# An attention block with modulation and experts: the loads and the first norms of its start in another order

## The chip, the cores and the metric

The kernel runs on one core of one Trainium2 chip. A core has TensorE (PE in the profile; its weight loads are the row PEld), VectorE (DVE), ScalarE (ACT), GpSimd (POOL) and SyncE (SP). Each works through its own instructions in order and waits on semaphores for the others. Transfers are issued by SP, ScalarE or GpSimd and run on 16 shared DMA engines. The metric is the device time of one execution in microseconds; lower is better.

## What is computed

The input x has 8 batches of 1024 tokens with 256 features. A small vector c per batch is turned into six rows of modulation (shift, scale and gate for each of two halves), which frame an attention with 16 heads of 64 and a layer of eight experts:

```python
mod = (_silu(c) @ wmod).reshape(8, 6, 1, -1)
sa, ca, ga, sb, cb, gb = (mod[:, i] for i in range(6))
ga = (2 * (ga >= 0) - 1) * jnp.maximum(jnp.abs(ga), 0.25)      # gb likewise
h = _layernorm(x) * (1 + ca) + sa
x = x + ga * attention(h, w_qkv, w_o)                          # softmax over 1024 keys, 16 heads
h = _layernorm(x) * (1 + cb) + sb
x = x + gb * experts(h, router_w, router_b, w1, b1, w2, b2)    # each expert takes its 512 best tokens
```

For the start of the kernel it matters who needs what. The first product (the values of the first heads of batch 0) needs the normalized x of batch 0, the shift and scale columns sa and ca, and the weights of a few heads. The gates and the second half's shift and scale are needed only when a whole batch has been through attention, and the router's weights and the experts' biases later still.

## The kernel before, in words

All arithmetic is in float32 apart from small helpers. Attention runs over units: a unit is one batch, one pair of heads and 512 of its 1024 queries (`unit`, L303). Per unit, eight chunks of 128 keys are multiplied to scores (`scores_mm`, L306), copied out by ScalarE (L322) while VectorE keeps the running maximum (L327), the maximum is turned and subtracted (L334 to L372), ScalarE takes the exponential (L375), TensorE multiplies with the values (L384), and GpSimd adds up the denominators (L403). Each batch also needs its x normalized and turned (`ln_task`: load L225, statistics L231, norm L234, transposes and modulation L243), and query, key and value products (`qk_task` L270, `v_task` L287).

The order of all this is written out by hand. `at(g, where, f)` puts a function into a table at step g, and the loop under `tc.manual_schedule()` (L647) runs through the steps, four to a unit; step 0 issues the first scores. Steps below 0 are the run-up: the loop starts at g = -28; batch 0's four pairs of token tiles are put at steps -23, -20, -17 and -14 (L604), each with its load four steps, its statistics two steps and its norm one step earlier; products of the first heads start at step -9 (L609 to L613).

Ahead of the loop stands a setup. SP issues rw, rb, b1 (L85, L87, L96) and then the whole of wmod (`wm`, L119). c becomes SiLU(c) in `silu`, is turned to `sT`, and is multiplied with wm in two forms: as columns, which give shift and scale of attention for each batch (`modT`, L134 to L141), and as rows, which give the two gates and the second shift and scale (`mrow`, L143 to L160), stored to DRAM as `mod_d` and `gb_d`. The setup has pools of its own, whose memory is given back before attention's pools are opened; so the query, key and value weights (`wq`, six transfers, L204) and `wo` (L208) are issued by ScalarE only after the setup's last use. They take the setup's place in memory.

A tile of a pool with a tag and `bufs` takes one of as many rotating buffers, and a new tile waits until the last use of the buffer that it takes is over. In PSUM, `ps_m` has a single buffer (tag "mm"), through which pass the transposes of the norm, the query, key and value products, the denominators and the output products. DMA completions are counted on eight semaphores in turn, so a transfer can also wait for the one eight places ahead of it.

The norm of one pair of tiles (`ln_norm`) takes rstd from two small GpSimd instructions (`rstd_of`, L166 and L168) and two GpSimd instructions for the norm itself (L238). `ln_out` makes 16 transposes on TensorE (L252) and two VectorE instructions that apply shift and scale (L257).

Of the kernel before, what the change touches and what calls it, by code (L numbers as in the profile page):

```python
# [28 lines left out]
F32 = mybir.dt.float32  # L29
BF16 = mybir.dt.bfloat16  # L30
I32 = mybir.dt.int32
AF = mybir.ActivationFunctionType
ALU = mybir.AluOpType
AX = mybir.AxisListType
PSUM = bass.MemoryType.PSUM
DRAM = bass.MemoryType.DRAM

P = 128
# [4 lines left out]
def adaln_block(  # L43
# [15 lines left out]
    nc = tc.nc  # L59
    B, S, D = x.shape  # L60
    H, _, _, N = w_qkv.shape
    E, _, F = w1.shape
    K = 512
    KC = D // P
    NT = S // P
# [7 lines left out]
    scale = 1.0 / N**0.5  # L73
# [4 lines left out]
    ident = const.tile([P, P], F32, name="ident")  # L78
# [3 lines left out]
    mhalf = const.tile([P, 1], F32, name="mhalf")  # L82
    nc.gpsimd.memset(mhalf, -0.5)
    rw = const.tile([P, KC, E], F32, name="rw")
    nc.sync.dma_start(rw, router_w.rearrange("(k p) e -> p k e", p=P))  # L85
    rb = const.tile([P, E], F32, name="rb")
    nc.sync.dma_start(rb, router_b.rearrange("(o e) -> o e", o=1).to_broadcast([P, E]))  # L87
    ident_b = const.tile([P, P], BF16, name="ident_b")
    nc.vector.tensor_copy(ident_b, ident)

# [2 lines left out]
    for j in range(2):  # L93
        nc.vector.memset(three[j * N : j * N + 3, :], 1.0)
    b1_sb = const.tile([P, E, FC], F32, name="b1_sb")
    nc.sync.dma_start(b1_sb, b1.rearrange("e (f p) -> p e f", p=P))  # L96

    scores = const.tile([P, KT, E, NTT // KT], F32, name="scores")
    modT = const.tile([P, 2 * KC, B], F32, name="modT")
# [10 lines left out]
    mod_d = dram.tile([B, 3 * D], F32, name="mod_d")  # L110
    gb_d = dram.tile([B, D], F32, name="gb_d")
    rows_d = dram.tile([B * S, WIDE], F32, name="rows_d")


    with tc.tile_pool(name="setup", bufs=1) as sp, tc.tile_pool(
        name="setup_ps", bufs=2, space=PSUM
    ) as spp:
        wm = sp.tile([P, KC, 6 * D], F32, name="wm")
        nc.sync.dma_start(wm, wmod.rearrange("(k p) m -> p k m", p=P))  # L119
        c_sb = sp.tile([B, D], F32, name="c_sb")  # L120
        nc.scalar.dma_start(c_sb, c)
        sig = sp.tile([B, D], F32, name="sig")
        nc.scalar.activation(sig, c_sb, AF.Exp, scale=-1.0)
        nc.vector.tensor_scalar_add(sig, sig, 1.0)
        nc.vector.reciprocal(sig, sig)
        silu = sp.tile([B, D], F32, name="silu")
        nc.vector.tensor_mul(silu, c_sb, sig)
        sT = sp.tile([P, KC, B], F32, name="sT")
        for k in range(KC):
            pt = spp.tile([P, B], F32, tag="small", name=f"pt{k}")  # L130
            nc.tensor.transpose(pt, silu[:, k * P : (k + 1) * P], ident[:B, :B])
            nc.vector.tensor_copy(sT[:, k, :], pt)

        for m in range(2 * KC):  # L134
            pm = spp.tile([P, B], F32, tag="small", name=f"pm{m}")
            for k in range(KC):
                nc.tensor.matmul(
                    pm, wm[:, k, m * P : (m + 1) * P], sT[:, k, :],
                    start=(k == 0), stop=(k == KC - 1),
                )  # L140
            nc.vector.tensor_scalar_add(modT[:, m, :], pm, 1.0 if m >= KC else 0.0)  # L141

        mrow = sp.tile([B, 4 * D], F32, name="mrow")  # L143
        for h in range(2):
            pr = spp.tile([B, 2 * D], F32, tag="row", name=f"pr{h}")
            for k in range(KC):
                nc.tensor.matmul(
                    pr, sT[:, k, :], wm[:, k, (2 + 2 * h) * D : (4 + 2 * h) * D],
                    start=(k == 0), stop=(k == KC - 1),
                )  # L150
            nc.vector.tensor_copy(mrow[:, 2 * h * D : (2 * h + 2) * D], pr)
        nc.vector.tensor_scalar_add(mrow[:, 2 * D : 3 * D], mrow[:, 2 * D : 3 * D], 1.0)
        for i in (0, 3):
            g = mrow[:, i * D : (i + 1) * D]
            sign = sp.tile([B, D], F32, name=f"sign{i}")
            nc.vector.tensor_scalar(sign, g, 0.0, 2.0, op0=ALU.is_ge, op1=ALU.mult)
            size = sp.tile([B, D], F32, name=f"size{i}")
            nc.vector.scalar_tensor_tensor(size, g, -1.0, g, op0=ALU.mult, op1=ALU.max)
            nc.vector.tensor_scalar_max(size, size, 0.25)
            nc.vector.scalar_tensor_tensor(g, sign, -1.0, size, op0=ALU.add, op1=ALU.mult)  # L160
        nc.sync.dma_start(mod_d, mrow[:, : 3 * D])
        nc.sync.dma_start(gb_d, mrow[:, 3 * D :])

    def rstd_of(pool, mv, n, name):
        ve = pool.tile([P, n], F32, tag="ve", name=f"ve_{name}")
# [16 lines left out]
    PB = 16  # L182
# [4 lines left out]
    wp = attn.enter_context(tc.tile_pool(name="wts", bufs=1))  # L187
    work = attn.enter_context(tc.tile_pool(name="work", bufs=2))
    small = attn.enter_context(tc.tile_pool(name="small", bufs=4))
# [2 lines left out]
    ps_av = attn.enter_context(tc.tile_pool(name="ps_av", bufs=1, space=PSUM))  # L192
    ps_m = attn.enter_context(tc.tile_pool(name="ps_m", bufs=1, space=PSUM))

    wq = wp.tile([P, KC, 3, H, N], F32, name="wq")
    wo = wp.tile([P, NP, D], F32, name="wo")

    parts_of = [wp.tile([P, 4, 2, N], BF16, name=f"parts{i}") for i in range(2)]
    for t in parts_of:
        nc.vector.memset(t, 0.0)  # L200

    for a in (2, 1, 0):
        for k in range(KC):
            nc.scalar.dma_start(  # L204
                wq[:, k, a],
                w_qkv[:, a, k * P : (k + 1) * P, :].rearrange("h p n -> p h n"),
            )
    nc.scalar.dma_start(wo, w_o.rearrange("(i p) d -> p i d", p=P))  # L208

    hTs, mods, qks, vs, oTs = {}, {}, {}, {}, {}  # L210
    tops, turned, rows_of, less, probs, sums, avs = {}, {}, {}, {}, {}, {}, {}
# [3 lines left out]
    def at(g, where, f, *args):  # L215
        steps.setdefault((g, where), []).append((f, args))
# [6 lines left out]
    ln_x = {}  # L223
# [7 lines left out]
    def ln_stats(b, t):  # L231
        ln_x[b, t] = ln_x[b, t], stats_of(small, ln_x[b, t], 2, f"a{b}_{t}")

    def ln_norm(b, t):  # L234
        xt, mv = ln_x[b, t]
        rs = rstd_of(small, mv, 2, f"a{b}_{t}")
        for i in range(2):
            nc.gpsimd.tensor_scalar(  # L238
                xt[:, i, :], xt[:, i, :], mv[:, i, 0:1], rs[:, i : i + 1],
                op0=ALU.subtract, op1=ALU.mult,  # L240
            )
# [21 lines left out]
    def ln_task(b, t, g):  # L263
        at(g - 4, "load", ln_load, b, t)
        at(g - 2, "post", ln_stats, b, t)
        at(g - 1, "pool", ln_norm, b, t)
        at(g, "m2", ln_out, b, t)


    def qk_task(b, p, i):  # L270
        a, half = (1, i) if i < 2 else (0, i - 2)
        if half == 0:
            qks[b, p, a] = work.tile([P, S], F32, tag="qk"[a], name=f"qk{a}_{b}_{p}")
        pq = ps_m.tile([P, 512], F32, tag="mm", name=f"pq{b}_{p}_{i}")
        sl = slice(half * 512, half * 512 + 512)
        for k in range(KC):
            for m in range(2):
                nc.tensor.matmul(  # L278
                    pq[m * N : (m + 1) * N, :], wq[:, k, a, 2 * p + m, :], hTs[b][:, k, sl],
                    start=(k == 0), stop=(k == KC - 1),  # L280
                )
        if a == 0:
            nc.scalar.mul(qks[b, p, a][:, sl], pq, scale)  # L283
        else:
            nc.scalar.copy(qks[b, p, a][:, sl], pq)  # L285

    def v_task(b, g, t):  # L287
        if t == 0:
            vs[b, g] = work.tile([P, NT, 4 * N], F32, tag="v", name=f"v{b}_{g}")
        pv = ps_m.tile([P, 2, 4 * N], F32, tag="mm", name=f"pv{b}_{g}_{t}")  # L290
        for i in range(2):
            for k in range(KC):
                for m in range(2):
                    t0 = (2 * t + i) * P + m * N
                    nc.tensor.matmul(  # L295
                        pv[m * N : (m + 1) * N, i, :], hTs[b][:, k, t0 : t0 + N],
                        wq[:, k, 2, 4 * g : 4 * g + 4, :],
                        start=(k == 0), stop=(k == KC - 1),
                    )
        nc.scalar.copy(vs[b, g][:, 2 * t : 2 * t + 2, :], pv)  # L300
# [300 lines left out]
        return g  # L601

    for t in range(NT // 2):
        ln_task(0, t, -23 + 3 * t)  # L604
        ln_task(1, t, free_slot(39 + 4 * t, True))
    for b in range(B):
        for p in range(NP):
# [13 lines left out]
        if b + 1 < B:  # L621
# [3 lines left out]
            for t in range(NT):  # L625
                g = free_slot(64 * (b + 1) + 19 + 4 * t, True)
# [3 lines left out]
                if t % 2:  # L630
                    g = free_slot(g + 2, True)
                    at(g, "m2", out_turn, ps_m, b, t - 1)
                    g = free_slot(g + 1)
# [7 lines left out]
            at(4 * u + 12, "m2", den_out, u)  # L641
    for b in range(B):
        at(64 * b + 30, "load", gates, b)
    for t in range(NT):
        at(4 * NSU + (3 if t < NT // 2 else 4), "load", last_load, t)

    with tc.manual_schedule():  # L647
        g = -28
        while g < 4 * NSU + LAG or steps:
            u, gm = divmod(g, 4)  # L650
            run(g, "load")
# [36 lines left out]
        b = B - 1  # L688
# [83 lines left out]
    with tc.tile_pool(name="search", bufs=2) as se, tc.tile_pool(  # L772
        name="pos", bufs=1
    ) as po_, tc.tile_pool(name="se_ps", bufs=2, space=PSUM) as sps, tc.tile_pool(
        name="pos_ps", bufs=1, space=PSUM
    ) as pps:
        for dst, pattern, mult in (
# [3 lines left out]
            i = po_.tile(list(dst.shape), I32, name=f"i_{dst.name}")  # L781
# [246 lines left out]
```

## Time and profile before

| | us |
| --- | --- |
| median of 3 runs | 3648.16 |
| lowest and highest | 3646.65 and 3648.54 |
| the profiled execution | 3645.84 |
| its span | 3644.1 |

| line | what | instructions | mean ns of one |
| --- | --- | --- | --- |
| L403 | POOL adds up denominators | 762 | 2371 |
| L372 | VectorE subtracts the maximum | 1024 | 1209 |
| L375 | ScalarE exponential | 1024 | 1057 |
| L322 | ScalarE copies scores | 1024 | 1018 |
| L313 | TensorE scores | 4096 | 613 |
| L384 | TensorE values | 4096 | 593 |
| L278 | TensorE queries and keys | 2048 | 605 |

The profile's page gives the busy time of each engine, then the span in 40 slices of equal length with the busy share of each engine in tenths, the clock that TensorE was granted, and the traffic. Busy matmul time is pipelined time: a full row says that TensorE always has something in progress. The timeline lists instructions in order of time; behind each stands, in brackets, how long its engine had been idle and what ended that. The mean granted clock of the execution was 0.979 of full speed.

### The profile page before, as it was taken

How to read it: one execution, taken by the hardware profiler on the slowest of the kernel's cores; microseconds unless marked ns; L12 is line 12 of the kernel's file. 1: busy time of each engine (PE TensorE's matmuls, PEld its weight loads, DVE VectorE, ACT ScalarE, POOL GpSimd, SP SyncE). 2: the span in 40 equal slices, each digit the busy share in tenths (PEclk: the TensorE clock that was granted, in tenths of full speed). 3: DMA queues.
4: the chain of work that ended last, by engine and by line, in shares of the span. 5: the costliest groups of instructions: out<-in, count | busy, mean ns of one | idle time of the engine just before them, and what ended most of it. 6: DMA issues, size and time to landing. Idle time of an engine off the chain costs nothing. (4 is left out here: it accounts for less than half of the span.)

```text
span 3644.1 us, 54310 instructions
## 1 busy us (share of the span) xinstructions
PE 3467.5 (95%) x20670; PEld 1461.3 (40%) x20670; DVE 2902.9 (80%) x3647; ACT 2431.7 (67%) x2978; POOL 2668.6 (73%) x1545
## 2 busy tenths in 40 slices
PE   5999999999999999999999999999999999982898
PEld 2333334334343444344343343344434334442565
DVE  3888888888888888888888888888888888857442
ACT  1777777777777777777777777777777777740111
POOL 1678777887788778888788888887888787851232
PEclk8999999999999999999999999999999999995999
DMA  3010002111120112011210113111211112133332
GB/s 76 7 39 27 24 31 58 49 38 45 45 62 30 52 48 66 29 45 45 62 52 29 51 50 62 30 50 46 62 38 43 46 48 59 51 85 122 93 99 41
DMA packets 189045, 185.40 MB, mean 51 GB/s; under 512 B 48856, under 2 KB 167144, under 8 KB 188656
## 3 DMA queue, kind: packets, MB, share of 16 engines
q1 hardware_dynamic: 159856, 156.62, 15.1%
q0 software_dynamic: 7168, 12.72, 1.7%
q10 hardware_dynamic: 21760, 12.59, 1.3%
q8 instruction: 163, 2.67, 0.3%
q14 instruction: 98, 0.80, 0.1%
HBM read 127.06 MB, written 63.21 MB: 52 GB/s over the span
## 5 line engine op out<-in xcount | busy, mean ns | idle before, releaser
L403 POOL TENSOR_TENSOR acc<-acc,p 128x1024 f32<-128x1024 f32 x762 | 1806.5, 2371 | 360.0 <-ACT p L375 327.0
L322 ACT COPY p<-s 128x1024 f32<-128x1024 f32 x1024 | 996.4, 1018 | 421.7 <-PE s L313 415.0
L372 DVE TENSOR_TENSOR p<-p,less 128x1024 f32<-128x1024 f32 x1024 | 1206.5, 1209 | 32.6 <-PE less L369 30.0
L327 DVE TENSOR_TENSOR top<-top,s 128x1024 f32<-128x1024 f32 x768 | 936.6, 1220 | 260.3 <-ACT p L322 219.3
L375 ACT ACTIVATE p<-p 128x1024 f32<-128x1024 f32 x1024 | 1041.8, 1057 | 74.7 <-DVE p L372 74.4
L313 PE MATMUL s<-qk,qk 64*128 64x512 f32 x4096 | 1025.8, 613 | 35.2 <-DVE parts L350 32.1
L384 PE MATMUL av<-p,v 128*64 128x512 f32 x4096 | 967.1, 593 | 1.8 <-ACT oT L393 1.8
L313 PEld LDWEIGHTS s<-qk,qk 64*128 64x128 f32 x4096 | 358.9, 187 | 527.4 <-issue 237.8
L278 PE MATMUL pq<-hT,wq 128*64 128x512 f32 x2048 | 495.9, 605 | 2.7 <-ACT qk L285 1.4
L384 PEld LDWEIGHTS av<-p,v 128*64 128x64 f32 x4096 | 280.6, 137 | 461.4 <-issue 366.9
L400 POOL TENSOR_TENSOR acc<-p,p 128x1024 f32<-128x1024 f32 x127 | 301.6, 2375 | 176.2 <-ACT p L375 176.2
L278 PEld LDWEIGHTS pq<-hT,wq 128*64 128x64 f32 x2048 | 124.2, 136 | 342.7 <-issue 211.4
L295 PE MATMUL pv<-wq,hT 128*64 128x256 f32 x2048 | 250.7, 387 | 2.6 <-ACT qk L283 1.4
L953 ACT ACTIVATE h<-ph,b_sb 128x512 f32<-128x512 f32 x64 | 44.0, 687 | 276.1 <-PE ph L949 276.1
L342 DVE TENSOR_REDUCE tt<-tt 128x8 f32<-128x1024 f32 x128 | 157.4, 1229 | 67.6 <-PE tt L334 67.5
L494 PE MATMUL po<-wo,ot 128*64 128x256 f32 x1792 | 205.7, 382 | 0.0
L295 PEld LDWEIGHTS pv<-wq,hT 128*64 128x64 f32 x2048 | 136.5, 137 | 155.7 <-issue 66.5
L327 DVE TENSOR_TENSOR top<-p,s 128x1024 f32<-128x1024 f32 x128 | 155.7, 1217 | 32.3 <-ACT p L322 32.3
L300 ACT COPY v<-pv 128x512 f32<-128x512 f32 x128 | 75.0, 586 | 148.4 <-PE pv L295 148.4
L334 PEld LDWEIGHTS tt<-ident,top 128*128 128x128 f32 x1024 | 109.6, 140 | 107.2 <-DVE top L327 107.2
L465 POOL TENSOR_TENSOR oT<-oT,rb 128x1024 f32<-128x1024 f32 x63 | 150.0, 2381 | 3.0 <-issue 3.0
L494 PEld LDWEIGHTS po<-wo,ot 128*64 128x64 f32 x1792 | 123.5, 137 | 66.2 <-issue 9.4
(161 smaller groups left out, 2442.8 us busy)
## 6 DMA issues: line engine op xcount, KB each, us to landing
rb<-rden_d SPq DMA_DIRECT2D x128, 256.0 KB
oT_d<-oT SPq DMA_DIRECT2D x62, 512.0 KB
ot<-oT_d SPq DMA_DIRECT2D x56, 512.0 KB
rows_d<-row SPq DMA_DIRECT2D x64, 132.0 KB
lnx<-in_L_attn_inputs_dram SPq DMA_DIRECT2D x32, 256.0 KB
rows_d<-gb_d SPq DMA_DIRECT2D x8, 1024.0 KB
w<-in_L_ffn_w_dram ACTq DMA_DIRECT2D x8, 1024.0 KB
w<-in_L_ffn_w_dram SPq DMA_DIRECT2D x8, 1024.0 KB
```

The costliest lines, as they stand in the source:

```text
L278: nc.tensor.matmul(pq[m * N : (m + 1) * N, :], wq[:, k, a, 2 * p + m, :], hTs[b][:, k, sl], start=(k == 0), stop=(k == KC - 1),)
L295: nc.tensor.matmul(pv[m * N : (m + 1) * N, i, :], hTs[b][:, k, t0 : t0 + N], wq[:, k, 2, 4 * g : 4 * g + 4, :], start=(k == 0), stop=(k == ...
L313: nc.tensor.matmul(ps[:, j, :], kt[r, c * P : (c + 1) * P], qt[r, h * QB : (h + 1) * QB], start=True, stop=True,)
L322: nc.scalar.copy(probs[u, c], ps)
L327: nc.vector.tensor_tensor(tops[u], probs[u, 0] if c == 1 else tops[u], ps, ALU.max)
L342: nc.vector.tensor_reduce(nm[:, 0, :], tt, AX.X, ALU.max, negate=True)
L372: nc.vector.tensor_tensor(probs[u, c], probs[u, c], less[u], ALU.add)
L375: nc.scalar.activation(probs[u, c], probs[u, c], AF.Exp)
L384: nc.tensor.matmul(avs[u][j * N : (j + 1) * N, :], v[:, c, hh * N : (hh + 1) * N], pT[:, j, :], start=(c == 0), stop=(c == NT - 1),)
L400: nc.gpsimd.tensor_tensor(sums[u], pts[0], pts[1], ALU.add)
L403: nc.gpsimd.tensor_tensor(sums[u], sums[u], pt, ALU.add)
L494: nc.tensor.matmul(po[m * N : (m + 1) * N, :], ot[:, p, m * N : (m + 1) * N], wo[:, p, :], start=(p == 0), stop=(p == NP - 1),)
```

## The change

- The transfers that the first products need are issued first. SP starts with c, the first 512 columns of wmod (shift and scale of attention) and the x of batch 0 in two halves; ScalarE starts with the weights of heads 0 to 3, six transfers.
- The weights of queries, keys and values are in two tiles: `wqs[0]` for four heads, `wqs[1]` for the other twelve. `wq_of` picks the right slice. The twelve heads, the other two thirds of wmod, wo, rw, rb and b1 follow on SP (`late_loads`).
- The setup has no memory of its own. Its tiles are put into buffers which attention uses later: wmod's first third and both halves of x in "p" buffers, wmod's other thirds in "ot", mrow in "rb", the small ones in "row", "dq", "ox" and "at". Its PSUM tiles go through `ps_m`.
- The norm of batch 0 runs ahead of the steps (`ln_first`), with its two instructions of a pair on VectorE. The other batches' stay on GpSimd. The transposes of batch 0 are at steps -15 to -12, and the loop starts at -16.
- The columns of modulation are multiplied into one PSUM tile and evacuated by two VectorE instructions (`mod_columns`). The rows (`mod_rows`) move to step -1, part "m2", which is after the third value product and ahead of the first scores; their evacuation is on ScalarE.

```diff
-    nc.sync.dma_start(rw, router_w.rearrange("(k p) e -> p k e", p=P))
...
-    nc.sync.dma_start(rb, router_b.rearrange("(o e) -> o e", o=1).to_broadcast([P, E]))
...
-    nc.sync.dma_start(b1_sb, b1.rearrange("e (f p) -> p e f", p=P))
...
-    with tc.tile_pool(name="setup", bufs=1) as sp, tc.tile_pool(
-        name="setup_ps", bufs=2, space=PSUM
-    ) as spp:
-        wm = sp.tile([P, KC, 6 * D], F32, name="wm")
-        nc.sync.dma_start(wm, wmod.rearrange("(k p) m -> p k m", p=P))
...
-    wq = wp.tile([P, KC, 3, H, N], F32, name="wq")
+    H0 = 4
+    wqs = [wp.tile([P, KC, 3, n, N], F32, name=f"wq{i}") for i, n in enumerate((H0, H - H0))]
...
+    c_sb = small.tile([B, D], F32, tag="row", name="c_sb", bufs=6)
+    nc.sync.dma_start(c_sb, c)
+    wm = [work.tile([P, KC, 2 * D], F32, tag=t, name=f"wm{i}", bufs=n)
+          for i, (t, n) in enumerate((("p", PB), ("ot", 2), ("ot", 2)))]
...
+    wm_load(0)
+    x_first = []
+    for i in range(2):
+        t = work.tile([P, NT // 2, D], F32, tag="p", name=f"x_first{i}", bufs=PB)
+        nc.sync.dma_start(
+            t, x[0, i * S // 2 : (i + 1) * S // 2, :].rearrange("(t p) d -> p t d", p=P)
+        )
+        x_first.append(t)
     for a in (2, 1, 0):
+        wq_load(nc.scalar, 0, a)
+
+    def late_loads():
+        for a in (2, 1, 0):
+            wq_load(nc.sync, 1, a)
+        for i in (1, 2):
+            wm_load(i)
+        nc.sync.dma_start(wo, w_o.rearrange("(i p) d -> p i d", p=P))
...
+    def mod_silu():
+        sig = small.tile([B, D], F32, tag="row", name="sig", bufs=6)
+        nc.scalar.activation(sig, c_sb, AF.Exp, scale=-1.0)
+        nc.vector.tensor_scalar_add(sig, sig, 1.0)
+        nc.vector.reciprocal(sig, sig)
+        nc.vector.tensor_mul(sig, c_sb, sig)
...
+    def mod_columns():
+        pm = ps_m.tile([P, 2 * KC, B], F32, tag="mm", name="pm")
...
+        nc.vector.tensor_copy(modT[:, :KC, :], pm[:, :KC, :])
+        nc.vector.tensor_scalar_add(modT[:, KC:, :], pm[:, KC:, :], 1.0)
+
+    def mod_rows(i):
...
+        pr = ps_m.tile([B, 2 * D], F32, tag="mm", name=f"pr{i}")
+        for k in range(KC):
+            nc.tensor.matmul(
+                pr, sT[:, k, :], wm[1 + i][:, k, :], start=(k == 0), stop=(k == KC - 1)
+            )
+        nc.scalar.copy(mrow[:, 2 * i * D : (2 * i + 2) * D], pr)
...
+    def ln_first(t):
+        ln_x[0, t] = x_first[t // 2][:, 2 * (t % 2) : 2 * (t % 2) + 2, :]
+        ln_stats(0, t)
+        ln_norm(0, t)
...
         for i in range(2):
-            nc.gpsimd.tensor_scalar(
+            eng = nc.vector if b == 0 else nc.gpsimd
+            eng.tensor_scalar(
...
-        ln_task(0, t, -23 + 3 * t)
+        at(-15 + t, "m2", ln_out, 0, t)
...
+    for i in range(2):
+        at(-1, "m2", mod_rows, i)
...
     with tc.manual_schedule():
-        g = -28
+        late_loads()
+        mod_silu()
+        ln_first(0)
+        mod_columns()
+        for t in range(1, NT // 2):
+            ln_first(t)
+        for t in parts_of:
+            nc.vector.memset(t, 0.0)
+        g = -16
```

## The prediction, made before the changed kernel was run

> **What bounds the kernel now.** I read the page first, then the timeline of the first 70 us, then windows of the granted clock, then ScalarE's transfer issues. From the page:
>
> ```profile
> PE 3467.5 (95%) x20670; PEld 1461.3 (40%) x20670; DVE 2902.9 (80%) x3647; ACT 2431.7 (67%) x2978; POOL 2668.6 (73%) x1545
> PE   5999999999999999999999999999999999982898
> PEclk8999999999999999999999999999999999995999
> ```
>
> A slice is 91 us. TensorE is full from the second slice to the end of attention; only the first is half empty. The change rewrites that first slice and no more: from the first scores on, every engine issues the same instructions in the same order as before, save a few split waits for the second half of the query/key/value weights. So whatever arrives at the first scores is carried to the end one for one, and the sum to make is when the first scores start. Timeline of the head (start, duration, engine, line, operation, idle time before and its releaser):
>
> ```profile
> 1.45 1.28 ACT L123 ACT_TABLE_LOAD   x1 [1.45 <-PEq L1014]
> 2.27 5.44 SPq L119 DMA_DIRECT2D wm<-in_L_wmod_dram  x1
> 2.74 0.41 ACT L123 ACTIVATE sig<-c_sb 8x256 f32<-8x256 f32 x1
> 13.87 0.57 PE L137 MATMUL pm<-sT,wm 128*128 128x8 f32 x2 [7.67 <-DMA wm<-in_L_wmod_dram]
> ...
> 16.89 2.45 POOL L238 TENSOR_SCALAR lnx<-lnx,mv_a,rs_a 128x256 f32<-128x256 f32 x2
> ...
> 47.39 1.54 PE L252 MATMUL ptx<-ident,lnx 128*64 128x128 f32 x12 [0.51 <-POOL lnx L238]
> 48.98 0.99 DVE L257 TENSOR_SCALAR hT<-ptx,modT 128x256 f32<-128x256 f32 x2 [5.25 <-PE ptx L252]
> ...
> 50.19 3.40 PE L295 MATMUL pv<-wq,hT 128*64 128x256 f32 x16 [1.25 <-issue]
> ...
> 69.28 1.99 PE L313 MATMUL s<-qk,qk 64*128 64x512 f32 x8
> 69.40 0.59 ACT L300 COPY v<-pv 128x512 f32<-128x512 f32 x1 [2.05 <-PE pv L295]
> ```
>
> TensorE first waits for wm (13.87), then four times for a normalized pair of token tiles from POOL (2.45 us each); the first value product starts at **50.19**, the first scores at **69.28**. The 19.09 us between are a chain of products and evacuations that the change keeps, with one thing put in at its end.
>
> **New first value product, part by part.** Let E be the end of the exponential in the SiLU (3.15 now).
>
> *VectorE to the transposed SiLU (S).* Add 0.28, reciprocal 1.74; then, ahead of the product in the new order, ident_b 0.21 and the 14 shifts 1.08, the product 0.41: E+3.8 with the gaps of now. Two transposes, each with a 0.17 copy, now in one PSUM buffer: about 0.55 each. S = E+4.9. The first x has landed by then (below).
>
> *Columns of the modulation.* 16 matmuls at 0.235 (the groups of six and eight took 1.45 and 1.88) and two copies of 0.17: S+4.3. Tile pair 0's norm fits beside it: statistics 1.17, POOL's rstd 1.1, two norms on VectorE at 0.41 (the last batch's out_norm, L517 on VectorE) make 3.1.
>
> *Norms.* VectorE's order has all four pairs before the first hT, and each waits for POOL's rstd in its middle: 3 more x 3.15 = 9.45, then the parts memsets 0.55: S+14.3. On POOL a pair's norm cost 2.45, here 0.82.
>
> *Transposes and hT.* Pair 0 was transposed meanwhile: hT 1.0. Pairs 1 to 3 are serial in the one PSUM buffer: transposes 2.07 (16 at the half-clock rate of the row at 47.39), hT 1.0, 0.15 of gaps: 3 x 3.22 = 9.65. The product follows 0.22 later: **S+25.2 = E+30.1**. Removing POOL's norm thus uncovers this serial chain; it is late next.
>
> *The clock.* Windows (engine columns, then granted clock, DMA share, GB/s):
>
> ```profile
> 24.00:26.00 2.00, 2.00 (x15) 1.33 (x16) 1.22 (x4) 0.00 (x0) 0.00 (x0) 1.00 0.00 0
> 30.00:40.00 10.00, 2.94 (x20) 1.74 (x20) 2.11 (x7) 0.00 (x0) 5.89 (x7) 0.50 1.01 216
> 52.00:53.00 1.00, 1.00 (x8) 0.67 (x6) 0.00 (x0) 0.00 (x0) 0.00 (x0) 0.50 0.00 0
> 54.00:56.00 2.00, 1.74 (x8) 0.48 (x8) 0.00 (x0) 0.20 (x1) 0.00 (x0) 1.00 0.00 0
> ```
>
> After the pause at 26.33 the clock fell to 0.5 and came back at 53, some 3 us into unbroken products. The new head has the same shape: TensorE pauses about 9 us between pair 0 and pair 1, so pairs 1 to 3 and the first product (3.40) run at half. [...] That speaks against the change, whose 16 column matmuls come after a long idle start: at half rate they cost 3.8 more. But this trace shows them at 1.00 after 13.8 us with two transposes only. [...]
>
> *E: what ScalarE issues first.* Its queue now begins with six transfers of 512 packets of 256 B (four heads of wq), then the table load 1.28, then the exponential 0.41. The present wq, 2048 such packets each:
>
> ```profile
> 29.65 2.06 ACTq L204 DMA_DIRECT2D wq<-in_L_attn_w_qkv_dram  x2
> 31.75 2.92 ACTq L204 DMA_DIRECT2D wq<-in_L_attn_w_qkv_dram  x1
> 34.71 2.10 ACTq L204 DMA_DIRECT2D wq<-in_L_attn_w_qkv_dram  x1
> ```
>
> The first issue took 0.41, later ones 1.6 to 2.9: an issue holds its engine until few packets of the ones before remain. How few: to 31.71 the queue moved 0.16 MB (628 packets), leaving 1420 of 2048; to 34.67 it moved 3440 of 4096, leaving 656; to 36.81 some 5118 of 6144, leaving 1030. So the sixth new issue, behind 2560 packets, ends when about 1530 (1140 to 1900) are moved. First packets 1.0 after the issue: 1.85. Alone 860 per us until wm's first third comes at about 2.5 (560); beside its 256 packets of 2 KB for 1.7 us I take 250 per us, between 81 (beside the experts' 4 KB packets, 323 in 4 us) and 440 (beside 1 KB ones, 530 in 1.2 us); 2 KB lies between the two sizes, so about the middle: 985 at 4.2. Beside x then 440: 1530 at 5.5 (4.6 to 6.3). E = 5.5+1.3+0.45 = **7.25** (6.35 to 8.1). [...] The rows decide, as they show ScalarE held.
>
> *SP's queue.* c_sb, wm's first 512 columns, x in two halves. In the old queue b1's 8192 packets of 4 B held wm back until 7.7; now b1 goes last. x's first half ends near 7, needed at S = 12.2; the second (its issue waits for the first wq part) near 10, needed at about 19.6. Transfers give cover of 5 us and more. The other heads, wm's rest, wo, rw, rb, b1 follow on SP: to wm's end 2.5 MB at about 390 GB/s and 3.0 MB of 256 B packets at 218: 20 us, so near 23.
>
> First value product: 7.25+30.1 = **37.3**, 12.9 earlier.
>
> **What is given back: the gates' rows.** They ran beside POOL's norm; now they stand between the last value product and the first scores (step -1), in the one PSUM buffer: wait for ScalarE's v copy 0.05+0.59+0.06, two matmuls of 8x512 1.88, ScalarE copy 0.05+0.58+0.06, two matmuls 1.81 to the next issue: 5.1. Queued behind on TensorE are all scores. Nine small VectorE operations (2.99 by the old rows) then stand ahead of the first running maximum, which is due 3.14 after the scores start; they end about 3.45 after: 0.3, passed on through the score buffer. Their stores on SP are needed much later. Together **5.4**.
>
> **Sum.** 12.9 - 5.4 = 7.4 us (unrounded terms). The profiled execution ran 3645.84 (span 3644.1, 1.7 around it) and would have span 3636.7; it lies 2.3 below the median of the runs, 3648.16, to which I apply the same difference: **3640.8**.
>
> **Rivals.**
> 1. ScalarE is not held (short transfers may slip through): E = 5.5, gain 9.2, 3639.0. For: the first 2048 were taken in 0.41. Against: the third and fourth issues. 0.22.
> 2. A longer head: cold column matmuls, or the table load, never seen here beside full queues, costing some 3 more: gain about 3.6 to 4.5, 3644.4. Against: clock 1.00 at 14 us. 0.21.
> 3. The gain doesn't arrive, because the first heads run on another engine's pace. For: POOL's accumulation waits only on ScalarE from 99 us on. Against: it is an effect of the same shifted start. 3648. 0.04.
> 4. Slower: the late loads. wm's last third is behind the 2.25 MB of other heads on SP. Landing at 23, it has cover until the gates' matmuls at 37.3+19.1 = 56.4. Each us past that delays the scores by one; from 63.8 the kernel is slower, at 70 it stands at 3654. It needs the 5.5 MB to move at under 90 GB/s. 0.03.
> The forecast itself: 0.50.
>
> **Numbers.** A difference of 0.2% (7.3 us) is about what this measurement tells from none; the forecast lies on it. Faster by more: half of the forecast and nearly all of rival 1: 0.49; slower 0.03; within 0.48. Range: from 11 us of gain (rival 1 with a warmer clock for pairs 1 to 3 and the first product, about 2) to 2.9 (rival 2 at its dear end, with the norms a little longer): 3637.2 to 3645.3.
>
> **What would show it.** Right: the exponential ends at 6.4 to 8.1, ScalarE's last wq issues are long, norms on VectorE 0.41, first value product at 36.5 to 38.2, 24.2 us from there to the first scores, and these near 61.5. Wrong: six issues of 0.45 (rival 1); column matmuls over 0.4 or a table load over 2 (rival 2); TensorE waiting for wm at step -1 (rival 4); a head that is earlier while the end is not (rival 3).

## The result, and the profile after

The changed kernel takes 3636.65 us, the median of 7 runs (3635.76 to 3640.74). The kernel before, run beside it, takes 3646.96 us (7 runs, 3646.65 to 3651.09). The ratio is 0.9971 with an interval of 0.9959 to 0.9982. So the change gains 10.3 us, or 9.15 us between the two profiled executions (3645.84 and 3636.69).

From the page of the changed kernel, busy time of the engines and the two rows by slices of 91 us:

```profile
PE 3462.8 (95%) x20670; PEld 1460.7 (40%) x20670; DVE 2904.0 (80%) x3651; ACT 2432.8 (67%) x2980; POOL 2657.6 (73%) x1537
PE   6999999999999999999999999999999999982898
PEclk9999999999999999999999999999999999995999
```

Only the first slice has changed: TensorE is busy for 62% of it (56.68 of 90.9 us) and was for 57% (51.99 of 91.1). The timeline of the head (start, duration, engine, line, operation, then the idle time before it and its releaser):

```profile
0.80 4.78 ACTq L157 DMA_DIRECT2D wq<-in_L_attn_w_qkv_dram  x6
...
5.62 1.28 ACT L201 ACT_TABLE_LOAD   x1 [5.62 <-issue]
...
6.91 0.41 ACT L201 ACTIVATE sig<-c_sb 8x256 f32<-8x256 f32 x1
...
11.98 3.58 PE L215 MATMUL pm<-sT,wm 128*128 128x8 f32 x16 [0.26 <-DVE sT L208]
...
23.85 0.73 DVE L281 TENSOR_SCALAR x_first<-x_first,mv_a,rs_a 128x256 f32<-128x256 f32 x2 [1.09 <-POOL rs_a L115]
24.59 0.55 DVE L700 MEMSET parts<- 128x256 uint32 x2
25.05 0.81 DVE L300 TENSOR_SCALAR hT<-ptx,modT 128x256 f32<-128x256 f32 x2
26.00 1.98 PE L295 MATMUL ptx<-ident,x_first 128*64 128x128 f32 x16 [8.06 <-DVE hT L300]
...
35.42 3.66 PE L338 MATMUL pv<-wq,hT 128*64 128x256 f32 x16 [1.18 <-DVE hT L300]
...
55.53 1.88 PE L229 MATMUL pr<-wm,sT 128*8 128x512 f32 x4 [0.68 <-ACT v L343]
57.45 0.57 ACT L232 COPY mrow<-pr 8x512 f32<-8x512 f32 x1 [1.97 <-PE pr L229]
58.08 1.88 PE L229 MATMUL pr<-wm,sT 128*8 128x512 f32 x4 [0.66 <-ACT mrow L232]
59.89 0.70 PE L356 MATMUL s<-qk,qk 64*128 64x512 f32 x2
```

A float32 matmul of the program stands in the trace as two records: the 8 that transpose a pair as x16, the 4 of the gates' rows as x8. Counts that are read from a trace are counts of records.

Read it in four stretches. ScalarE issues transfers until 5.58 and only then makes the SiLU. VectorE then makes all four norms, the last one ending at 24.58, before the first hT at 25.05, while TensorE waits 8.06 us. After that comes a chain of transposes and hT. The first value product starts at 35.42 in place of 50.19 (-14.77), and after the gates' rows the first scores start at 59.89 in place of 69.28 (-9.39).

The rest carries this to the end unchanged. The fourth score chunk starts at 64.67 in place of 73.69, the first maximum is turned at 76.20 in place of 85.23 (both -9.0), and the span is 9.1 shorter. The 0.4 between -9.39 and -9.0 are the nine VectorE operations of the gates: the first running maximum follows the first scores by 3.52 us, where it followed by 3.14.

### The profile page after: what moved, and what is told of

Read it like the earlier page. It is cut to its first block, busy times and chain, and to the rows that moved or that the text cites. A ratio compares the mean times of both kernels' runs of the same rounds, so it can differ in the third digit from the quotient of the medians.

```text
span 3635.0 us, 54304 instructions
## 1 busy us (share of the span) xinstructions
PE 3462.8 (95%) x20670; PEld 1460.7 (40%) x20670; DVE 2904.0 (80%) x3651; ACT 2432.8 (67%) x2980; POOL 2657.6 (73%) x1537
```

## The experiments

Each kernel was run beside the kernel before. "Value product" and "scores" are the starts of the first ones in the profile, "distance" is the time from one to the other. These three are from one profiled execution each, and the end of the exponential alone lies between 7.04 and 7.91 in the runs that leave its place as in the changed kernel, so half a microsecond between two runs says little. The last two columns compare with the executions of the kernel before that ran beside that kernel; the medians of those lie between 3645.21 and 3646.96.

| run | value product | distance | scores | median us | less than before | ratio and interval |
| --- | --- | --- | --- | --- | --- | --- |
| before | 50.19 | 19.09 | 69.28 | 3646.96 | | |
| after | 35.42 | 24.47 | 59.89 | 3636.65 | 10.3 | 0.9971 (0.9959 to 0.9982) |
| exp_first | 30.35 | 24.42 | 54.77 | 3631.45 | 13.8 | 0.9961 (0.9947 to 0.9975) |
| norm_on_pool | 30.66 | 27.96 | 58.62 | 3633.05 | 12.2 | 0.9963 (0.9950 to 0.9975) |
| norms_between | 31.44 | 26.24 | 57.68 | 3632.94 | 13.9 | 0.9958 (0.9942 to 0.9975) |
| warm_head | 32.51 | 22.76 | 55.27 | 3632.66 | 14.2 | 0.9958 (0.9942 to 0.9975) |
| norm_on_pool_warm | 30.86 | 22.78 | 53.64 | 3629.19 | 17.6 | 0.9953 (0.9936 to 0.9969) |
| rows_early | 35.11 | 19.22 | 54.33 | 3629.72 | 15.5 | 0.9957 (0.9941 to 0.9974) |
| before_b1_late | 46.13 | 19.08 | 65.21 | 3641.05 | 4.2 | 0.9988 (0.9979 to 0.9997) |
| before_order_alone | 42.87 | 22.87 | 65.74 | 3639.14 | 7.6 | 0.9977 (0.9969 to 0.9986) |
| before_vector_norm_alone | 45.23 | 19.38 | 64.61 | 3641.14 | 5.6 | 0.9986 (0.9979 to 0.9992) |
| combination | 16.48 | 18.44 | 34.92 | 3610.84 | 36.0 | 0.9899 (0.9882 to 0.9915) |

### ScalarE's transfers ahead of the exponential

The exponential is issued first, the six transfers behind it.

```diff
-    for a in (2, 1, 0):
-        wq_load(nc.scalar, 0, a)
...
     with tc.manual_schedule():
-        late_loads()
         mod_silu()
+        for a in (2, 1, 0):
+            wq_load(nc.scalar, 0, a)
+        late_loads()
```

> The changed kernel with ScalarE's table load and exponential issued ahead of the six transfers of the first heads' weights. Theory A (the sixth issue holds ScalarE until the packets before it are moved, and the exponential heads the chain): exponential ends near 2.7 to 3.0 in place of 7.32, first value product earlier by 3.8 to 4.5 us (the first half of x, which lands near 7, may take up to 0.5 of it), first scores near 55.6. Theory B (the arrival of x or of wm sets the head anyway): first value product within 1 us of 35.42.

The timeline of exp_first:

```profile
0.80 1.28 ACT L198 ACT_TABLE_LOAD   x1 [0.80 <-PEq L1066]
...
2.29 0.41 ACT L198 ACTIVATE sig<-c_sb 8x256 f32<-8x256 f32 x1 [0.21 <-DMA c_sb<-in_L_c_dram]
2.30 7.29 ACTq L157 DMA_DIRECT2D wq<-in_L_attn_w_qkv_dram  x6
...
30.35 3.60 PE L335 MATMUL pv<-wq,hT 128*64 128x256 f32 x16 [1.14 <-issue]
```

The exponential ends at 2.70 in place of 7.32, and the value product and the scores follow 5.07 and 5.12 earlier. The six issues now hold ScalarE for 7.29 us and nobody waits for it. So six issues ahead of the exponential cost about 5 us. Only part of this is the hold: in the changed kernel the first four issues took 0.44 to 0.53 each and the last two 0.90 and 1.71, some 1.6 more than two of the others would have (an estimate from these figures).

### The gates' rows in TensorE's pause

The row products follow the transposes of pair 0, in buffers of the scores. Their part of wmod is loaded ahead of the other heads, and the nine VectorE operations stand at step -7.

```diff
+        for i in (1, 2):
+            wm_load(i)
         for a in (2, 1, 0):
             wq_load(nc.sync, 1, a)
...
-        pr = ps_m.tile([B, 2 * D], F32, tag="mm", name=f"pr{i}")
+        pr = ps_s.tile([B, 2 * D], F32, tag="s", name=f"pr{i}")
...
+        if t == 0:
+            for i in range(2):
+                at(-15, "m2", mod_rows, i)
...
-    for i in range(2):
-        at(-1, "m2", mod_rows, i)
+    at(-7, "post", mod_gates)
```

> The changed kernel with the two row products of the modulation and their ScalarE copies directly behind the transposes of pair 0, in the score buffers, which are idle then; wm's other thirds are loaded ahead of the twelve heads, and the nine VectorE operations stand at step -7. Theory A (step -1 costs 5.4 us, and TensorE has an 8 us pause between pair 0 and pair 1 that takes the matmuls): first scores 5.0 to 5.5 us earlier than changed relative to the first value product (distance 24.47 becomes 19.1), first scores near 54.5; at the half clock the two row products take 3.8 each and may push pair 1 by up to 0.5. Theory B (the first scores wait for something else at step -1, such as the last key product's copy): distance stays above 23.

The timeline of rows_early:

```profile
18.44 4.99 PE L229 MATMUL pr<-wm,sT 128*8 128x512 f32 x8
...
26.57 1.09 PE L296 MATMUL ptx<-ident,x_first 128*64 128x128 f32 x16 [3.15 <-DVE hT L301]
28.80 1.97 PE L296 MATMUL ptx<-ident,x_first 128*64 128x128 f32 x16 [1.14 <-issue]
```

The rows fit into the pause. The distance is 19.22, which is 5.25 less, and the scores start 5.56 earlier. So the place at step -1 costs what the prediction said. The two rows of transposes, 1.09 and then 1.97 for the same 16, were a surprise: see the clock below.

### Which engine makes the norm, and where it stands

Four runs. In the first the two instructions of a norm go back to GpSimd and the rest of the change stays.

```diff
-            eng = nc.vector if b == 0 else nc.gpsimd
+            eng = nc.gpsimd
```

> The changed kernel with batch 0's norms on GpSimd as before (L281); all else as changed. In the changed kernel the first scores start at 59.89 us and the first value product at 35.42. Theory A (the norms on VectorE are not what gains: VectorE takes its work in order, so the hT of pair 0 stands behind all four norms, and the transposes run one after the other after that): on GpSimd the pairs take 3.6 us each (rstd 1.1, norm 2.45) but VectorE is free for hT by about 20, so that transposes and norms overlap; last norm ends near 27.7, first value product near 31.0, first scores near 55.5, about 4.4 us earlier than changed. Theory B (a pair's norm at 0.73 in place of 2.45 is part of the gain): first scores later by up to 4 x 1.7 = 6.9 us, near 66.8.

In the second they stay on VectorE, but pairs 2 and 3 come behind the hT of pairs 0 and 1.

```diff
         at(-15 + t, "m2", ln_out, 0, t)
+        if t < 2:
+            at(-15 + t, "m2", ln_first, t + 2)
...
-        for t in range(1, NT // 2):
-            ln_first(t)
+        ln_first(1)
```

> The changed kernel, norms still on VectorE, but pairs 2 and 3 have statistics and norm after the shift and scale (hT) of pairs 0 and 1 instead of ahead of them. Theory A (what held the value product in the changed kernel is VectorE's order, four norms ahead of the first hT, not the engine of the norm): transposes of pairs 1, 2, 3 near 20.5, 24.4, 28.3, value product near 31.5 (-3.9); the clock may stay low longer, so first scores 53 to 57. Theory B (VectorE is too slow for the norms wherever they stand, GpSimd is needed): value product within 1 us of 35.4.

The timeline of norms_between, VectorE and the product:

```profile
19.72 0.81 DVE L300 TENSOR_SCALAR hT<-ptx,modT 128x256 f32<-128x256 f32 x2
...
22.69 0.74 DVE L281 TENSOR_SCALAR x_first<-x_first,mv_a,rs_a 128x256 f32<-128x256 f32 x2 [1.09 <-POOL rs_a L115]
...
26.50 0.74 DVE L281 TENSOR_SCALAR x_first<-x_first,mv_a,rs_a 128x256 f32<-128x256 f32 x2 [1.09 <-POOL rs_a L115]
...
31.44 3.68 PE L338 MATMUL pv<-wq,hT 128*64 128x256 f32 x16 [1.18 <-DVE hT L300]
```

In both runs the first hT starts near 19.7 instead of 25.05, and the value product gains 4.76 and 3.98 (forecast in the expectation: 31.5, measured 31.44). So it is the order on VectorE that holds the product in the changed kernel, and the engine of the norm decides little there. But only 1.27 and 2.21 of that reach the scores. The timeline of norm_on_pool shows where the rest stays:

```profile
30.66 3.68 PE L338 MATMUL pv<-wq,hT 128*64 128x256 f32 x16 [1.19 <-DVE hT L300]
...
35.02 3.68 PE L321 MATMUL pq<-hT,wq 128*64 128x512 f32 x8 [0.68 <-ACT v L343]
...
39.38 3.66 PE L321 MATMUL pq<-hT,wq 128*64 128x512 f32 x8 [0.69 <-ACT qk L328]
...
43.73 1.94 PE L321 MATMUL pq<-hT,wq 128*64 128x512 f32 x8 [0.69 <-ACT qk L328]
```

Three products take twice their usual 1.94. In the changed kernel only one did (3.66 at 35.42), in norms_between two. The profiled execution of norms_between is the slowest of its four (3635.73, median 3632.94), so its others may have lost less.

The other two runs make parts of the change in the kernel before. One puts the norm on VectorE there.

```diff
-            nc.gpsimd.tensor_scalar(
+            eng = nc.vector if b == 0 else nc.gpsimd
+            eng.tensor_scalar(
```

> The kernel before with the norm's two instructions of batch 0 on VectorE and nothing else changed. Theory A (the ring above): each turn of the ring loses about 2.45 - 0.74 us less some 0.4 because the transposes no longer start behind the first half, so 3 turns give about 4: value product near 46.2, first scores near 65.3, time near 3642. Theory B (VectorE's norm is what gains in the changed kernel): value product before 42, time 3638 or less. Theory C (a slower VectorE queue eats it): no gain.

The other only moves the statistics and the norm ahead of the hT of the pair before.

```diff
-        ln_task(0, t, -23 + 3 * t)
+        g = -23 + 3 * t
+        at(g - 5, "load", ln_load, 0, t)
+        at(g - 4, "post", ln_stats, 0, t)
+        at(g - 4, "pool", ln_norm, 0, t)
+        at(g, "m2", ln_out, 0, t)
```

> The kernel before, norms on GpSimd and transfers as they were, but each pair of batch 0 has its load one step, its statistics two and its norm three steps earlier, so that they stand ahead of the shift and scale (hT) of the pair before it on VectorE instead of behind it. Theory A (what spaced the pairs 7.33 us apart was that ring: hT, statistics, rstd, norm, transposes, hT, closed by the order on VectorE): the ring is cut, pairs 1 to 3 follow at about the 3.6 us of GpSimd or the arrival of their x, first value product near 40 (-10), first scores near 59 (-10) if the clock does as before, time near 3636. Theory B (GpSimd's speed at the norm, or a late x, spaced them): value product later than 46 (less than 4 us gained).

The value product gains 4.96 in the first and 7.32 in the second. In the kernel before, hT, the next pair's statistics, rstd, norm, transposes and hT were one ring. One turn of it, in the kernel before:

```profile
34.33 0.99 DVE L257 TENSOR_SCALAR hT<-ptx,modT 128x256 f32<-128x256 f32 x2 [4.23 <-PE ptx L252]
...
35.24 0.42 DVE L176 BATCH_NORM_STATS2 st_a<-lnx 128x6 f32<-128x256 f32 x1
...
37.58 2.43 POOL L238 TENSOR_SCALAR lnx<-lnx,mv_a,rs_a 128x256 f32<-128x256 f32 x2
...
40.06 1.55 PE L252 MATMUL ptx<-ident,lnx 128*64 128x128 f32 x12 [0.51 <-POOL lnx L238]
41.66 0.99 DVE L257 TENSOR_SCALAR hT<-ptx,modT 128x256 f32<-128x256 f32 x2 [5.25 <-PE ptx L252]
```

A turn takes 7.33 us, so a faster norm shortens it and a different order cuts it. The second run fell short of the 10 expected. Its timeline shows what took over:

```profile
29.75 0.40 SPq L227 DMA_DIRECT2D lnx<-in_L_attn_inputs_dram  x1
...
35.07 0.43 DVE L176 BATCH_NORM_STATS2 st_a<-lnx 128x6 f32<-128x256 f32 x1 [3.81 <-DMA lnx<-in_L_attn_inputs_dram]
...
42.87 3.68 PE L295 MATMUL pv<-wq,hT 128*64 128x256 f32 x16 [1.42 <-issue]
```

The x of pair 3, issued beside the head weights, is waited for until 35.07, 5.3 us after its issue, where pair 2's took 2.7 (25.90 to 28.60). That the weights' transfers slow it fits, but no run takes them away. With only two buffers for x it could not be issued earlier. Of the 7.3 gained, the profiled run keeps 3.5 at the scores, again because of products at half speed (three in a row take 3.68, at 42.87, 47.23 and 51.59). Its 12 runs lie between 3635.10 and 3642.06. The clock goes with that: the three with a mean granted clock of 0.981 or 0.982 took 3635.10 to 3637.24, the nine with 0.980 took 3637.57 to 3642.06.

### The clock in the head

> The changed kernel with matmuls added whose result nothing reads: 28 of 128x128 after the transposes of tile pair 0 of batch 0, and 4 after those of each later pair, in a spare score buffer, so that TensorE doesn't stand still while VectorE makes the norms. Theory A (the head's transposes and first product ran at half clock, although the record shows 1.00 before its first event): transposes of pairs 1 to 3 near 1.09 us each in place of 1.97, the first value product 1.95 in place of 3.66, so value product near 32.8, first scores near 55.5 (-4.0 to -4.5), time near 3632.5. Rival B (the record of 1.00 is true and these rows are slow for another reason, such as waiting for the weights of each): rows of 1.97 and 3.66 as before, first scores 59.9 or later, time 3637 or more.

Here matmuls whose result nothing reads fill TensorE's pauses; no other instruction changes.

```diff
+    def keep_busy(t, n):
+        spare = ps_s.tile([P, P], F32, tag="s", name=f"spare{t}")
+        for _ in range(n):
+            nc.tensor.matmul(spare, ident, ident, start=True, stop=True)
...
         at(-15 + t, "m2", ln_out, 0, t)
+        at(-15 + t, "m2", keep_busy, t, 28 if t == 0 else 4)
```

Windows of one microsecond in warm_head, all within one run of like matmuls (busy time and number started of TensorE, weight loads, VectorE, ScalarE and GpSimd, then granted clock, DMA share, GB/s):

```profile
17.60:18.60 1.00, 1.00 (x7) 1.00 (x5) 0.83 (x3) 0.00 (x0) 0.13 (x1) 1.00 1.35 218
18.60:19.60 1.00, 1.00 (x7) 1.00 (x7) 0.91 (x4) 0.00 (x0) 0.00 (x0) 1.00 1.34 217
19.60:20.60 1.00, 1.00 (x12) 1.00 (x11) 0.00 (x0) 0.00 (x0) 0.85 (x2) 1.00 1.34 218
20.60:21.60 1.00, 1.00 (x12) 1.00 (x11) 0.93 (x3) 0.00 (x0) 0.03 (x1) 1.00 1.25 225
```

From 19.6 on twelve matmuls start per microsecond, before that seven, and the granted clock reads 1.00 throughout, so the 1.00 ahead of 19.6 doesn't tell how fast TensorE ran there. From 19.6 on the timeline of the same run is fast:

```profile
25.73 1.09 PE L295 MATMUL ptx<-ident,x_first 128*64 128x128 f32 x16 [0.74 <-DVE hT L300]
...
32.51 1.95 PE L338 MATMUL pv<-wq,hT 128*64 128x256 f32 x16
```

The scores start at 55.27, 4.62 earlier, as theory A said (55.5). The same filling on top of norm_on_pool (9, 10, 10 and 6 of them):

> The norms of batch 0 on GpSimd, as in norm_on_pool, with spare matmuls after each pair's transposes (9, 10, 10, 6). Theory A (that kernel's first scores came only 4.8 - 3.5 us earlier because its pauses kept the clock low until 42.9): GpSimd's last norm again ends near 27.9 and the value product starts near 30.0, now at full clock (1.95), so the first scores come 22 to 23 us after it, near 52.7, span near 3628. Rival B (the longer way from the value product to the scores has another cause): distance near 28, first scores near 58, span near 3632.

The distance falls from 27.96 to 22.78, and the scores start at 53.64. All distances with the rows at step -1 now follow from one price: 22.76 with every product at full speed, and 1.73 more for each that runs at half (3.68 against 1.95). One gives 24.5 (after: 24.47), two 26.2 (norms_between: 26.24), three 28.0 (norm_on_pool: 27.96).

### The small transfers at the head of SP's queue

In the kernel before, rw, rb and b1 are issued at step -2 and nothing else changes.

```diff
-    nc.sync.dma_start(rw, router_w.rearrange("(k p) e -> p k e", p=P))
...
-    nc.sync.dma_start(b1_sb, b1.rearrange("e (f p) -> p e f", p=P))
...
+    at(-2, "load", late_loads)
```

> The kernel before with one thing changed: rw, rb and b1 are issued by SP at step -2 in place of at the start. Theory A (b1's 8192 packets of 4 bytes held back wm until 7.7 us, and wm heads the chain of the old head): first modulation product near 7.5 in place of 13.87, first value product near 44, first scores near 63 (6.2 us earlier). Theory B (GpSimd's norms alone pace the old head): first scores within 1 us of 69.28.

The timeline of before_b1_late:

```profile
9.79 0.60 PE L134 MATMUL pm<-sT,wm 128*128 128x8 f32 x2 [3.54 <-DVE sT L129]
...
46.13 3.37 PE L292 MATMUL pv<-wq,hT 128*64 128x256 f32 x16 [1.25 <-DMA wq<-in_L_attn_w_qkv_dram]
```

TensorE no longer waits for wm, and the columns start 4.08 earlier; beyond that VectorE's copies of the SiLU stand behind the statistics of pair 0, which wait for x until 8.11, so the 6.2 expected did not come. The value product and the scores gain 4.06 and 4.07, all that the columns gained. Which of the three transfers does it was not taken apart.

### All of it together

The last kernel joins what the runs point to: exponential first, x ahead of wmod, wmod's other thirds ahead of the other heads, the four pairs transposed in four separate PSUM buffers before the hT, constants and memsets behind the first value product, and the gates' row products one by one in the gaps of the product chain.

```diff
-        ln_first(0)
+        for a in (2, 1, 0):
+            wq_load(nc.scalar, 0, a)
+        late_loads()
+        first_stats(0)
+        first_stats(1)
+        ln_norm(0, 0)
         mod_columns()
-        for t in range(1, NT // 2):
-            ln_first(t)
-        for t in parts_of:
-            nc.vector.memset(t, 0.0)
-        g = -16
+        ln_norm(0, 1)
+        turned_x = [ln_turn(0, 0, ps_m, "mm"), ln_turn(0, 1, ps_av, "av")]
+        first_stats(2)
+        first_stats(3)
+        for t in (2, 3):
+            ln_norm(0, t)
+            turned_x.append(ln_turn(0, t, ps_s, "s"))
+        for t in range(NT // 2):
+            ln_mod(0, t, turned_x[t])
+        g = -10
...
+    for j, g in enumerate((-9, -7, -6, -5)):
+        at(g, "m2", mod_rows, j // 2, j % 2)
+    at(-8, "post", constants)
+    at(-4, "post", mod_gates)
```

> All that the runs point to in one kernel: x loaded ahead of wmod's first third, exponential ahead of ScalarE's transfers, wmod's other thirds ahead of the other heads, the statistics of both tiles of x's first half ahead of the norms, the four pairs' transposes in four separate PSUM buffers, hT after them, constants and memsets behind the first value product, the gates' row products one by one in the gaps of the product chain (steps -9 to -5), their VectorE operations at step -4. Norms on VectorE. If the terms add up: value product near 19.5, first scores near 40 (-20), time 3616 to 3618. Rivals: the clock stays low through the head (+3 to 5 us), or the transfers of x and weights set the end instead (scores at 45 or later, time 3622 or more).

The timeline of the combination:

```profile
7.02 3.56 PE L209 MATMUL pm<-sT,wm 128*128 128x8 f32 x16 [1.19 <-DVE st_a L118]
...
10.50 3.25 PE L304 MATMUL ptx<-ident,x_first 128*64 128x128 f32 x32
...
14.14 2.26 PE L304 MATMUL ptx<-ident,x_first 128*64 128x128 f32 x32 [0.39 <-DVE x_first L288]
...
16.48 1.95 PE L353 MATMUL pv<-wq,hT 128*64 128x256 f32 x16
...
34.92 1.99 PE L371 MATMUL s<-qk,qk 64*128 64x512 f32 x8
```

It beats both kernels: 3610.84 us, 36.0 below the kernel before and 25.8 below the changed one. The expectation was 3616 to 3618. Of the 5.1 more at the scores, 3.0 are there at the value product and 2.1 lie in the distance. No run takes these parts alone; the timeline shows that TensorE has no pause of its own any more between 7.02 and 13.75. The second half of the transposes takes 2.26 where the first took 3.25, the value, query and key products from 16.48 to 27.77 take the 1.94 and 1.95 of full speed, and the row products (1.02 and 1.03 each) stand in gaps in which TensorE would wait for ScalarE's copies. The distance is 18.44, shorter than the 19.09 of before, with the rows in it.

## Why the prediction missed, step by step

The forecast was 3640.8 with a range down to 3637.2; the median is 3636.65. The mechanisms that the sum was built on were at work. The step that failed is the last one, from the profile to the median: it added 2.3 us, and the changed kernel's profiled execution lies on its median. The second term that was off is VectorE's part of the head, a set of small durations that came to 1.9 us too much.

- **ScalarE held (right).** The exponential ends at 7.32 against 7.25 forecast. The six issues took 4.78 us, singly 0.44, 0.53, 0.53, 0.53, 0.90 and 1.71. The forecast was right to go by the rows of long issues: the 5.5 for E of rival 1 did not occur, and exp_first, which puts the exponential ahead of all six issues, gains 5.07. Rival 1 falls, though its time, 3639.0, lies nearer to the result; it gets there by a mechanism that wasn't there.
- **First value product (37.3 forecast, 35.42 measured: mis-sized).** The step "3 more x 3.15 = 9.45" with its neighbours is too long. A pair's period is 2.92, because a pair of norms takes 0.73 (at about 0.41 each the forecast took 0.82) and the statistics and rstd overlap a little more. Of the 1.9 us, 1.2 lie between the transposed SiLU and the first hT, 0.3 in the SiLU itself, 0.2 in the first hT, 0.3 in the chain of transposes and hT; E gave 0.1 back. No single term is off by much, but nearly all are off the same way.
- **What held the first pair before (wrong).** The forecast has TensorE wait four times for a normalized pair from POOL, and the old row products run beside POOL's norm. For pairs 1 to 3 the first is so. For pair 0 it isn't: its norm ended at 19.34, and TensorE, working in order, came to its transposes only behind the last row products.

```profile
21.16 3.58 PE L147 MATMUL pr<-wm,sT 128*8 128x512 f32 x4
...
24.68 1.65 PE L252 MATMUL ptx<-ident,lnx 128*64 128x128 f32 x16
...
26.46 0.53 DVE L257 TENSOR_SCALAR hT<-ptx,modT 128x256 f32<-128x256 f32 x1
```

  So the rows were not free in the old head: without them those transposes could have started up to 5.3 us earlier (an estimate from 19.34 and 24.68). The forecast did not need this term, since it sums the new head from its start.
- **What becomes late next (half right).** The serial chain through the one PSUM buffer is there as forecast. Ahead of it stood VectorE's order, counted in the sum but not named as a choice: norms_between takes 3.98 off the value product by order alone.
- **The clock (right size, wrong reasoning).** The forecast read the granted clock of 1.00 at 14 us as full speed for the column products and left the 3.8 of half rate to rival 2. The rows show half: in the kernel before, a row product (two records) among the column products took 1.88 at 14.36 and 17.55, where one takes 1.02 at 18.35 in the combination. So the 1.00 was not a measurement; in the trace of before the first clock event lies at 25.9, behind all column products. But the durations in the sum (0.235 a column product) came from the same cold stretch, so the half rate was in them already, and adding 3.8 would have counted it twice: 16 column products took 3.58. Rival 2 falls: its cold columns were no new cost, and the table load beside full queues took its usual 1.28.
- **Gates' rows (right).** 5.4 was forecast. At full speed the distance is 22.76 with the rows at step -1; in rows_early it is 19.22 with one product still slow by 1.57, so the rows cost 5.1, and VectorE's part adds little: the first maximum follows the scores by 3.52 against 3.45 forecast. Within this, "two matmuls of 8x512 1.88" was right by luck: that row was one matmul at half speed, and two at full speed take the same.
- **Cover of the transfers (right).** Columns, statistics and rows start without waiting for a DMA. Rival 4 falls.
- **Carried to the end (right).** The scores gain 9.39 and the span 9.1. Rival 3 falls.
- **From the profile to the median (wrong).** "it lies 2.3 below the median of the runs, 3648.16, to which I apply the same difference". The changed kernel's profiled execution, 3636.69, lies on its median, and more runs put the median of before at 3646.96. The sum itself said 3645.84 - 7.4 = 3638.4. So of the 4.1 between forecast and result, 2.4 are this step and 1.7 are the head. An offset between one execution and three runs is scatter: of 31 later executions of the kernel before, the ten with a mean granted clock of 0.980 took 3643.96 to 3645.92, the seven with 0.978 took 3647.71 to 3649.56. The range was counted from 3648.16 too, and that is why it missed: its gains of 2.9 to 11 hold the measured 10.3, and counted from 3646.96 it would have reached down to 3636.0.

What made the gain: the two heads side by side show where it lies. The column products start 1.89 us earlier (11.98 for 13.87), the transposes of pair 0 8.72 earlier (15.96 for 24.68), the first hT only 1.41 earlier (25.05 for 26.46), the first value product 14.77 earlier. So 13.4 of the 14.8 lie between the first hT and the value product, where the ring was. What was gained ahead of the first hT was spent again on six issues ahead of the exponential and on four norms in a row on VectorE, each worth 4 to 5 us at the value product, which the experiments took back.

Alone, in the kernel before, the small transfers cost 4.1 at the scores (before_b1_late) and the ring 4.7 with a faster norm (before_vector_norm_alone), or 7.3 at the value product when its order is changed (before_order_alone). The rows cost 5.1 at their new place; what they cost at their old one, no run takes alone. The parts overlap, so they don't add up to the whole.

## What to carry to other kernels

When the head of a kernel is carried to the end one for one, treat it as a chain of its own: look at what stands ahead of each instruction in its engine's order, and move out everything that the first product does not need, transfer issues on a computing engine included (six of them ahead of the exponential cost 5.07 us at the value product, by exp_first). Look for pauses of TensorE in the head, and put useful products into them: here that saved the 5.25 us of the rows at step -1 (rows_early), and filled pauses brought the full clock forward (warm_head, where the same transposes took 1.09 in place of 1.97). When a step is priced from rows, ask at which clock those rows ran before a half clock is added to them: the 3.58 of the column products had it in already.

## What the runs showed of the hardware

**A reading and a duration.** In warm_head the granted clock reads 1.00 from 17.6 to 21.6, while TensorE starts 7 matmuls a microsecond and from 19.6 on 12 of the same kind; 16 records of transposes take 1.97 at 15.68 and 1.09 at 25.73. The first clock event of the trace lies at 25.9 in the kernel before and at 38.9 in the changed one. Ahead of it the reading is 1.00 in both, and slow rows stand there: 3.58 for two row products at 21.16 in the kernel before, where two take 1.88 at 55.53 in the changed one; 1.97 for a pair's transposes at 29.11 and 3.66 for the value product at 35.42 in the changed one. So in these traces a reading ahead of that event says nothing, and the durations of like rows do.

**How long the slow rows lasted.** From the first column product to the first rows at full speed it took at most 7.1 us in the combination (7.02 to 14.14) and 7.9 in warm_head (11.71 to 19.6), but 31.7 in norm_on_pool (12.08 to 43.73).

**Pauses.** In norm_on_pool TensorE pauses for 1.19 to 2.19 us ahead of each pair's transposes from the second on and ahead of the value product, and for 0.68 and 0.69 between the three slow products that follow (3.68, 3.68 and 3.66). In norm_on_pool_warm, where matmuls fill the pauses from the first transposes at 16.05 to the end of the value product, those transposes take 2.15, the next 1.09 from 21.40 on, and the value product 1.95. So the filling brought the full clock. How short the pauses must be for that, or how busy TensorE, was not shown.

**The way down.** In the kernel before TensorE stops at 26.33, and the granted clock reads 0.95 from 29.0 to 29.3 and 0.50 from 29.3 to 30.0. In rows_early TensorE pauses for 3.15 us up to 26.57. The transposes there still take 1.09; the next, at 28.80, take 1.97, and the clock reads 0.52 from 28 to 30.
